# The second half of a quantized feed-forward layer: chunk loads moved from ScalarE's DMA queue to SyncE's, with another ring of integers and another split of the rounding

## The chip, the cores and the metric

The kernel runs on one core of a Trainium2 chip (trn2). The metric is the device time of one execution in microseconds; less is better. Five engines run their own instruction streams in order: TensorE (PE, its weight loads PEld), VectorE (DVE), ScalarE (ACT), GpSimd (POOL) and SyncE (SP). SP computes nothing; it issues DMAs. ACT can issue DMAs too. An instruction that waits holds up everything behind it on its engine, and this holds for SP's queue as well.

## The reference, cut to what matters

Two batches of 2048 tokens with 512 features pass through four residual steps. The last one, `_L1_ffn_ref`, is the part concerned:

```python
def act_quant(x):
    scale = 127.0 / jnp.clip(jnp.max(jnp.abs(x), axis=-1, keepdims=True), 1e-05)
    return jnp.clip(jnp.round(x * scale), -128, 127) / scale
...
h = bit_linear(x, w1)                 # 512 -> 2048, ternary weights
h = depthwise_conv1d(h.transpose(0, 2, 1), conv_w, conv_b)   # three taps along the tokens
h = h.transpose(0, 2, 1)
h = jax.nn.silu(h)
return bit_linear(h, w2)              # 2048 -> 512, ternary weights
...
x = x + jnp.tanh(g_xattn[1]) * _L1_xattn_ref(_layernorm(x, axis=-1), ctx_768, ...)
x = x + jnp.tanh(g_ffn[1]) * _L1_ffn_ref(_layernorm(x, axis=-1), ...)
```

`bit_linear` quantizes each token's row to integers of at most 127 before it multiplies. The scale of the second `bit_linear` needs the largest absolute value over all 2048 hidden features of a token, so nothing of a token's second half can be quantized until its whole first half is known.

## The kernel before

Tokens go in eight blocks of 512, g0 to g7, four to a batch (`NBLK` = 4, `LAST` = 7). The hidden features go in 16 chunks of 128 (`HC` = 16); a chunk of a block is a tile of 128 features by 512 tokens.

Beside the last attention (stage 3) runs the **first half** of each block, `first_half(g)`: for each chunk four matmuls (L1002), a scaling on DVE (L1012), the middle tap of the convolution on ACT (L1014), the two outer taps on DVE (L1018), all in `convolved`. After four chunks ACT applies Silu (L1043), SP stores the 1 MB of four chunks to DRAM (`h_d[g]`, L1049), ACT takes the absolute value in place (L1050, which must wait for that store), and DVE folds the maximum (L1051 to L1056). `quantize_rows(g)` makes the block's input: normalize and scale the four x3 tiles (ACT L968 and L978, DVE L971 and L980 into `xi`), and transpose them on PE (L986). g7 is not stored: its four-chunk tiles stay in SBUF (`kept`).

`scales_of(g)` turns the maxima into scales: a PE transpose (L1073), a DVE reduction (L1075) and five DVE instructions on four columns. For g0 to g3 (`EARLY` = 4) the integers are made during the attention by `integers(g)` and stored as bf16 in `hq_d[g]`. For g4 to g7 `quantize_hidden(g)` makes them in the second half.

The **second half** of a block, from `second_half_starts()` on, is in `down_and_out`: for each of the block's four row tiles 16 matmuls with the integers as weights (L1232), DVE scales and adds the residual (L1235), SP stores the result (`out_x`, L1236). Residual rows come from `x3_d` by `row_tile` (L1162); since the convolution lags one token, the first row tile of each batch (g0 and g4) has 127 rows, and its load and its store are DMAs of 127 rows.

`quantize_hidden(g)` before the change: for g0 to g3 it loads eight bf16 tiles of two chunks (`hq`, 256 KB each, L1198, by SP). For g4 to g6 it loads two chunks at a time (512 KB, L1188) by ACT's queue into six `h5` buffers, four loads ahead; multiplies by the scale spread over the partitions (`s_b`, one buffer, written by ACT at L1086) on DVE, every fourth on POOL (L1207); then rounds by adding and subtracting a large constant, odd ones on ACT in two steps (L1212, L1213), even ones on DVE in one (L1215). The integer tiles lie in two sets of eight, by the block's parity. `xr` holds eight x3 buffers, which in stage 3 carry the attention's residual rows, four to a block.

The order on each engine is not the program's: a scheduler places each instruction, and all waits go through semaphores. DMAs of SP and ACT take turns in eight completion slots; a DMA waits until the one eight before it has landed.

Of the kernel before, what the change touches and what calls it, by code (L numbers as in the profile page):

```python
# [10 lines left out]
F32 = mybir.dt.float32  # L11
BF16 = mybir.dt.bfloat16
AF = mybir.ActivationFunctionType
ALU = mybir.AluOpType
# [3 lines left out]
P = 128  # L18
B, S, D = 2, 2048, 512
NT = B * S // P  # L20
TPB = S // P
BLK = 512
TB = BLK // P
NBLK = S // BLK
# [8 lines left out]
HC = HID // P  # L33
# [5 lines left out]
def row_tiles(ap):  # L39
    return ap.rearrange("(c p) n -> p c n", p=P)  # L40
# [3 lines left out]
def flamingo_kernel(ctx: ExitStack, tc: tile.TileContext, a: dict, out: bass.AP):  # L44
    nc = tc.nc
# [4 lines left out]
    def psum_pool(stack, name, bufs):  # L50
        return stack.enter_context(tc.tile_pool(name=name, bufs=bufs, space=PSUM))
# [340 lines left out]
    with ExitStack() as st:  # L392
# [17 lines left out]
            out=before,  # L410
            in_=before,
# [9 lines left out]
            out=after,  # L421
            in_=after,
# [174 lines left out]
    with ExitStack() as st:  # L597
        AHEAD = 3
        wst = st.enter_context(tc.tile_pool(name="wst", bufs=AHEAD))
        keepp = st.enter_context(tc.tile_pool(name="keepp", bufs=1))  # L600
        w13 = {}

        def load_ffn(f):
            n = min(P, DFF - f * P)
            w1c = wst.tile([P, DC, P], F32, name="w1c", tag="w1c")
            nc.sync.dma_start(
                out=w1c[:, :, :n], in_=row_tiles(a["W1T"])[:, :, ds(f * P, n)]
            )
            w2c = wst.tile([P, DC, P], F32, name="w2c", tag="w2c")
            nc.sync.dma_start(  # L610
                out=w2c[:, :, :n], in_=row_tiles(a["W2T"])[:, :, ds(f * P, n)]
            )
            w3c = wst.tile([P, D], F32, name="w3c", tag="w3c")
            nc.sync.dma_start(out=w3c[:n, :], in_=a["W3T"][ds(f * P, n), :])
            w13[f] = (w1c, w2c, w3c)
# [28 lines left out]
        with ExitStack() as sa:  # L644
# [9 lines left out]
            for n in range(3):  # L654
                nc.sync.dma_start(
                    out=wqkv[:, :, ts(n, D)], in_=row_tiles(a["WqkvT"])[:, :, ts(n, D)]
                )
            wout = w.tile([P, DC, D], F32, name="wout")
            nc.sync.dma_start(out=wout, in_=row_tiles(a["WoutT"]))
            for f in range(AHEAD):  # L660
                load_ffn(f)
# [131 lines left out]
        with ExitStack() as sf:  # L793
# [64 lines left out]
            def down(f):  # L858
                n = min(P, DFF - f * P)
                for i in range(4):  # L860
                    nc.tensor.matmul(  # L861
                        acc[i],
                        gT[f][:n, ts(i, P)],
                        w13[f][2][:n, :],
                        start=(f == 0),
                        stop=(f == NF - 1),
                    )

            for f in range(NF):
# [16 lines left out]
                if f > 0:  # L886
                    down(f - 1)
                    if f - 1 + AHEAD < NF:
                        load_ffn(f - 1 + AHEAD)
                if f == 1:  # L890
# [8 lines left out]
            for i in range(4):  # L899
# [3 lines left out]
                    out=x_d[i // 2][:, :],  # L903
                    out_offset=bass.IndirectOffsetOnAxis(ap=idx[:, i : i + 1], axis=0),
                    in_=xa[i],
# [14 lines left out]
    GC = 4  # L920
# [7 lines left out]
    h_d = [dramp.tile([P, HC, BLK], F32, name=f"h_d{g}") for g in range(B * NBLK)]  # L928
    LAST = B * NBLK - 1
# [7 lines left out]
    xr = s4.enter_context(tc.tile_pool(name="xr", bufs=8))  # L937
# [4 lines left out]
    def quant_scale(mx, name, s=None):  # L942

        m = row4.tile([P, TB], F32, name=name + "m", tag="qm")
        nc.vector.tensor_scalar(m, mx, 1e-5, None, ALU.max)
        if s is None:
            s = row4.tile([P, TB], F32, name=name + "s", tag="qs")
        nc.vector.reciprocal(s, m)
        nc.vector.tensor_scalar(s, s, 127.0, None, ALU.mult)
        inv = row4.tile([P, TB], F32, name=name + "i", tag="qi")  # L950
        nc.vector.reciprocal(inv, s)
        return s, inv
# [42 lines left out]
    carry, ending, kept, act5 = {}, [], [], []  # L995
# [70 lines left out]

    def scales_of(g, amax):

        for _ in range(3):
            yield  # L1070
        pm = ps_mm.tile([P, TB, P], F32, name="pm", tag="mm")
        for i in range(TB):
            nc.tensor.transpose(pm[:, i, :], amax[:, ts(i, P)], ident)  # L1073
        mx = row4.tile([P, TB], F32, name="mxh", tag="mx4")
        nc.vector.tensor_reduce(mx, pm, AX.X, ALU.max)  # L1075
        _, inv = quant_scale(mx, "hq", hid_s[:, ts(g, TB)])
        nc.vector.tensor_scalar(hid_f[:, ts(g, TB)], inv, finstep, None, ALU.mult)
        if g < EARLY:
            later.append(integers(g))

    def scales_spread(g):

        pb = ps_mm.tile([P, BLK], F32, name="pb5", tag="mm")
        bcast_rows(pb, hid_s[:, ts(g, TB)], ident)
        s_b = act4.tile([P, BLK], F32, name="s_b", tag="s_b", bufs=1)
        nc.scalar.copy(s_b, pb)  # L1086
        return s_b
# [29 lines left out]
    def beside4(u, share=2):  # L1117


        for _ in range(share):  # L1120
            advance(ending)
            advance(stream)
        if u is None or u % 4 != 1:
            advance(later)
# [23 lines left out]


    w5, ps_5, quantizing, ahead = [], [], [], []  # L1150
    GQ, hq, used = 2, {}, []

    def row_tile(g, i):

        t = w5[0].tile([P, D], F32, name="x5w", tag="x5w", bufs=2)
        if g + i > 1:
            t = act5[0].tile([P, D], F32, name="x5", tag="x5", bufs=8)
        r, p = g % NBLK * BLK + i * P - 1, 0
        if r < 0:
            nc.sync.dma_start(out=t[0:1, :], in_=x3_d[g // NBLK][0:1, :])  # L1160
            r, p = 0, 1
        nc.sync.dma_start(out=t[p:, :], in_=x3_d[g // NBLK][ds(r, P - p), :])  # L1162
        return t, r, p

    def second_half_starts():
        units.close()
        w5.append(s4.enter_context(tc.tile_pool(name="w5", bufs=1)))
        w5.append(w5[0].tile([P, HC, D], BF16, name="w2q"))
        quantizing.append(quantize_hidden(0))
        nc.sync.dma_start(out=w5[1], in_=w2_d)  # L1170
        ps_5.append(psum_pool(s4, "s5_o", 4))
        next(quantizing[0], None)
        ahead.extend(row_tile(0, i) for i in range(2))

    def quantize_hidden(g):

        NK = HC // GQ
        hq[g] = []

        def load(k):  # L1180
            if g == LAST:
                return kept[k * GQ // GC][:, ds(k * GQ % GC, GQ), :]
            pool = (act5 if len(used) % 3 else w5)[0]
            used.append(g)
            h = pool.tile(
                [P, GQ, BLK], F32, name="h5", tag="h5", bufs=4 if pool is act5[0] else 2
            )
            nc.scalar.dma_start(out=h, in_=h_d[g][:, ts(k, GQ), :])  # L1188
            return h

        def integer_tile():
            pool = act5[0] if g % 2 else w5[0]
            hq[g].append(pool.tile([P, GQ, BLK], BF16, name="hq", tag="hq", bufs=NK))
            return hq[g][-1]

        if g < EARLY:
            for k in range(NK):
                nc.sync.dma_start(out=integer_tile(), in_=hq_d[g][:, ts(k, GQ), :])  # L1198
            return
        AHEAD = 4  # L1200
        hs = [load(k) for k in range(AHEAD)]
        s_b = scales_spread(g)
        yield
        for k in range(NK):
            h = hs.pop(0)
            eng = nc.gpsimd if k % 4 == 3 else nc.vector
            eng.tensor_tensor(  # L1207
                h, h, s_b.unsqueeze(1).to_broadcast([P, GQ, BLK]), ALU.mult
            )
            q = integer_tile()  # L1210
            if k % 2:
                nc.scalar.activation(h, h, AF.Copy, bias=RND)  # L1212
                nc.scalar.activation(q, h, AF.Copy, bias=-RND)  # L1213
            else:
                nc.vector.tensor_scalar(q, h, RND, RND, ALU.add, ALU.subtract)  # L1215
            if k + AHEAD < NK:
                hs.append(load(k + AHEAD))
            yield

    cross_attention(  # L1220
        W1, act, hold, ps_mm, psum_pool(units, "L1_sc", 3), psum_pool(units, "L1_o", 2), row,
# [52 lines left out]
    for g in range(LAST + 1):  # L1274
        if g == LAST - 1:
            while stream or ending:
                beside4(None)
            last_tokens()
        behind = quantize_hidden(g + 1) if g < LAST else iter(())
        for i in range(TB):  # L1280
            t, r, p = ahead.pop(0)
            down_and_out(
                lambda c: hq[g][c // GQ][:, c % GQ, ts(i, P)],
                hid_f[:, g * TB + i : g * TB + i + 1],
                P,
                t,
                out[ds(g // NBLK * S + r, P - p), :],
                p,
            )
            if g < LAST:  # L1290
                ahead.append(row_tile(g + 1, i))
            for _ in range(3):
                next(behind, None)
                beside4(None, 1)
# [65 lines left out]
```

## Time and profile before

| what | value |
|---|---|
| median of 3 runs | 1890.75 us (1885.45 to 1895.94) |
| profiled execution | 1896.89 us, its span 1892.8 us |
| mean TensorE clock granted | 0.945 |
| first L1012 of g7's first half | 1739.1 us after the start of the span |
| first L1207 (g4) | 1790.8 us |
| h loads by ACT | 24 of 512 KB, median 6.0 us from issue to landing |
| x5 and residual row loads by SP | 60 of 256 KB, median 5.1 us |
| L1207 on DVE, on POOL | 24 of 1479 ns, 8 of 2957 ns |
| L1212 and L1213 on ACT | 16 of 1052 ns, 16 of 1054 ns |

A group line of the profile reads: line, engine, operation, output <- input (partitions x elements, type), count | busy us, mean ns of one | idle time of the engine just before these instructions, with what ended it. A stretch line reads: from:to, length, then for each engine busy us and count, the granted TensorE clock, the DMA engines' busy share, and GB/s. In the views the tiles `x3` and `x5` both appear as `x`, `x3_d` and `x_d` as `x_d`, and `h5` as `h`.

### The profile page before, as it was taken

What the parts mean: (1) busy time and instruction counts of PE and PEld (TensorE: products, weight loads), DVE (VectorE), ACT (ScalarE), POOL (GpSimd) and SP (SyncE); (2) the same over time, 40 slices, a digit from 0 to 9 for tenths busy, and PEclk for the clock granted to TensorE, in tenths of its full rate; (3) what the DMA queues carried; (4) which work ended last, traced back from release to release, by engine and by line L of the source; (5) the groups of instructions that cost most, each with busy time, mean ns of one, the idle gap of its engine ahead of it and who ended that gap; (6) DMA issues with size and microseconds to landing.
All of it is one profiled execution on the core that took longest, in us unless ns stands there. A gap on an engine that the chain in (4) does not pass through costs nothing.

```text
span 1892.8 us, 24174 instructions
## 1 busy us (share of the span) xinstructions
PE 1684.2 (89%) x7580; PEld 841.7 (44%) x7626; DVE 1312.3 (69%) x2713; ACT 1041.1 (55%) x3021; POOL 554.0 (29%) x676
## 2 busy tenths in 40 slices
PE   6989988888837989989999999999999999887877
PEld 4544544444313543445544444445444444433433
DVE  5777898878772432224447789799798789675956
ACT  1645545355402635205547778788787779643523
POOL 4534343343202310032214242323234233221212
PEclk9999999899958989999999999999999999898989
DMA  7011011011122019330011134234243133157463
GB/s 281 1 45 46 1 46 45 12 45 46 45 94 100 1 62 347 110 89 23 29 40 62 78 117 142 98 123 150 75 143 101 78 103 131 36 210 239 154 220 127
DMA packets 94998, 184.33 MB, mean 97 GB/s; under 512 B 10944, under 2 KB 30144, under 8 KB 91159
## 3 DMA queue, kind: packets, MB, share of 16 engines
q1 hardware_dynamic: 90518, 168.11, 25.5%
q10 hardware_dynamic: 3456, 12.58, 2.0%
q0 software_dynamic: 896, 2.10, 0.6%
q8 instruction: 60, 0.98, 0.2%
q14 instruction: 68, 0.55, 0.1%
HBM read 108.31 MB, written 74.45 MB: 97 GB/s over the span
## 4 chain that ended last, share of the span: by engine, by line
PE 37%; DVE 12%; DMA 6%; ACT 4%; issue 2%; POOL 2%; SPq 1%; ACTq 0%; DVEq 0%; POOLq 0%
PE pp L315 9%; PE pq L248 8%; PE ph L1002 3%; PE po L297 3%; PE sc L271 3%; DVE h L1018 2%; PE pu L875 2%; PE tp L289 2%; PE po L1232 2%; PE acc L861 2%; PE pw L875 2%; DMA h<-h_d 1%; DVE h L1207 1%; DMA out_x<-x 1%; DMA out_x<-x5w 1%
## 5 line engine op out<-in xcount | busy, mean ns | idle before, releaser
L128 POOL TENSOR_TENSOR A<-A,rden 128x512 f32<-128x512 f32 x280 | 298.2, 1067 | 552.4 <-DVE rden L127 448.6
L119 ACT ACTIVATE A<-sc,nmx 128x128 f32<-128x128 f32 x1024 | 362.8, 377 | 168.5 <-DVE nmx L116 145.8
L315 PE MATMUL pp<-L_wo,OT 128*128 128x512 f32 x768 | 366.1, 611 | 10.2 <-DVE x L324 6.8
L248 PE MATMUL pq<-xnT,L_wq 128*128 128x512 f32 x768 | 360.6, 616 | 0.0
L119 ACT ACTIVATION_READ_ACCUMULATOR A<-sc,nmx 128x1 f32 x1024 | 221.4, 216 | 0.0
L248 PEld LDWEIGHTS pq<-xnT,L_wq 128*128 128x128 f32 x768 | 146.1, 197 | 161.2 <-issue 153.3
L116 DVE TENSOR_REDUCE nmx<-sc 128x4 f32<-128x512 f32 x256 | 169.1, 677 | 67.1 <-PE sc L271 66.8
L290 DVE COPY AT<-tp 128x512 f32<-128x512 f32 x256 | 172.9, 677 | 56.5 <-PE tp L289 56.0
L315 PEld LDWEIGHTS pp<-L_wo,OT 128*128 128x128 f32 x768 | 138.9, 195 | 157.8 <-issue 135.1
L1018 DVE SCALAR_TENSOR_TENSOR h<-u,cw,h 128x512 f32<-128x512 f32 x256 | 190.7, 779 | 6.0 <-ACT h L1014 5.5
L289 PE MATMUL tp<-ident,A 128*128 128x128 f32 x1024 | 164.5, 283 | 28.3 <-POOL A L128 26.7
L271 PE MATMUL sc<-L_kT,qT 32*128 32x128 f32 (+1 forms) x2048 | 163.5, 290 | 5.8 <-ACT A L119 5.1
L271 PEld LDWEIGHTS sc<-L_kT,qT 32*128 32x128 f32 (+1 forms) x2048 | 130.4, 188 | 85.5 <-issue 60.8
L289 PEld LDWEIGHTS tp<-ident,A 128*128 128x128 f32 x1024 | 119.7, 143 | 103.0 <-issue 47.5
L1232 PE MATMUL po<-w2q,hq 128*128 128x512 bf16 x501 | 125.9, 406 | 37.6 <-DMA hq<-hq_d 12.8
L1014 ACT ACTIVATE h<-u,cb,cw 128x512 f32<-128x512 f32 x128 | 99.1, 809 | 59.3 <-DVE u L1012 52.3
L1002 PE MATMUL ph<-xiT,w1q 128*128 128x512 bf16 x477 | 122.4, 380 | 6.0 <-DVE u L1012 3.9
L297 PE MATMUL po<-AT,L_v 128*32 128x512 f32 (+1 forms) x512 | 118.8, 634 | 9.4 <-DVE AT L290 9.0
L305 ACT COPY OT<-po 128x512 f32<-128x512 f32 x96 | 55.8, 588 | 103.2 <-PE po L297 102.7
L1012 DVE TENSOR_TENSOR u<-ph,inv_b 128x512 f32<-128x512 f32 x128 | 85.0, 682 | 33.0 <-PE ph L1002 26.1
L1011 POOL COPY u<-carry 128x2 f32<-128x2 f32 x128 | 49.1, 386 | 200.1 <-DVE h L1018 171.7
L1232 PEld LDWEIGHTS <-hq 128*128 128x128 bf16 x512 | 51.2, 103 | 108.9 <-issue 23.4
(218 smaller groups left out, 2266.3 us busy)
## 6 DMA issues: line engine op xcount, KB each, us to landing
h_d<-h SPq DMA_DIRECT2D x28, 1024.0 KB, 4.1
x_d<-x SPq DMA_DIRECT2D x64, 256.0 KB, 2.0
hf<-h_d SPq DMA_DIRECT2D x64, 256.0 KB, 3.0
x<-x_d SPq DMA_DIRECT2D x60, 256.0 KB, 5.1
h<-h_d ACTq DMA_DIRECT2D x24, 512.0 KB, 6.0
x<-in_x SPq DMA_DIRECT2D x32, 256.0 KB, 5.4
xn_d<-xn SPq DMA_DIRECT2D x32, 256.0 KB, 2.2
xf<-x_d SPq DMA_DIRECT2D x32, 256.0 KB, 3.0
```

What stands on the lines that cost most here:

```text
L116: nc.vector.tensor_reduce(nmx, sc, AX.X, ALU.max, negate=True)
L119: nc.scalar.activation(out_tile[:, h, :], sc[:, h, :], AF.Exp, bias=nmx[:, h : h + 1], accum_out=den[:, h : h + 1],)
L128: nc.gpsimd.tensor_tensor(out_tile, out_tile, rden.unsqueeze(2).to_broadcast([P, n, width]), ALU.mult,)
L248: nc.tensor.matmul(pq, W.wq[:, d, ts(e, P)], xnT[:, d, :], start=(d == 0), stop=(d == DC - 1),)
L271: nc.tensor.matmul(sc[h][:, t, :], qT[e % cpg][r, ts(t, P)], W.kT[r, b, e, :], start=True, stop=True,)
L289: nc.tensor.transpose(tp[:, t, :], A[:, t, :], ident)
L290: nc.vector.tensor_copy(AT, tp.rearrange("p t n -> p (t n)"))
L297: nc.tensor.matmul(po[h * dh : (h + 1) * dh, :], W.v[:, b, ts(hd, dh)], AT[c * hpc + h], start=True, stop=True,)
L315: nc.tensor.matmul(pp, OT[e][:, ts(i, P)], W.wo[:, e, :], start=(e == 0), stop=(e == nE - 1),)
L1002: nc.tensor.matmul(ph, w1q[:, d, ts(c, P)], xiT[g][:, d, :], start=(d == 0), stop=(d == DC - 1),)
L1018: nc.vector.scalar_tensor_tensor(z, u[:, ds(k, BLK)], cw[:, c, k : k + 1], z, ALU.mult, ALU.add)
L1232: nc.tensor.matmul(po, rows(c), w2q[:, c, :], start=(c == 0), stop=(c == HC - 1))
```

## The change

The integers of g0 and g1 are both requested when the second half starts, g1's second four tiles at the generator's next step. Integer tiles come from one ring of 24 (three blocks), twelve in each of two pools. For g4 to g6, single chunks (256 KB) are loaded by SP into the `x3` buffers, six ahead. All scaling is on DVE in tiles of 512, for g7 too. Of four chunks, one is rounded on DVE and three on ACT. `scales_of(6)` waits 16 turns of its generator instead of 3. The condition on where the first row tiles lie takes in the block size.

```diff
     def scales_of(g, amax):
-        for _ in range(3):
+        for _ in range(3 if g != LAST - 1 else HC):
             yield
...
-    GQ, hq, used = 2, {}, []
+    GQ, hq = 2, {}
+    next_integers = iter(range(B * NBLK * HC // GQ))
 
     def row_tile(g, i):
         t = w5[0].tile([P, D], F32, name="x5w", tag="x5w", bufs=2)
-        if g + i > 1:
+        if g * TB + i > 1:
             t = act5[0].tile([P, D], F32, name="x5", tag="x5", bufs=8)
...
-        quantizing.append(quantize_hidden(0))
         nc.sync.dma_start(out=w5[1], in_=w2_d)
         ps_5.append(psum_pool(s4, "s5_o", 4))
-        next(quantizing[0], None)
+        quantizing.extend(quantize_hidden(g) for g in range(2))
+        for q in quantizing:
+            next(q, None)
         ahead.extend(row_tile(0, i) for i in range(2))
 
     def quantize_hidden(g):
-        NK = HC // GQ
         hq[g] = []
-        def load(k):
-            if g == LAST:
-                return kept[k * GQ // GC][:, ds(k * GQ % GC, GQ), :]
-            pool = (act5 if len(used) % 3 else w5)[0]
-            used.append(g)
-            h = pool.tile(
-                [P, GQ, BLK], F32, name="h5", tag="h5", bufs=4 if pool is act5[0] else 2
-            )
-            nc.scalar.dma_start(out=h, in_=h_d[g][:, ts(k, GQ), :])
-            return h
-
         def integer_tile():
-            pool = act5[0] if g % 2 else w5[0]
-            hq[g].append(pool.tile([P, GQ, BLK], BF16, name="hq", tag="hq", bufs=NK))
+            pool, bufs = (w5[0], 12) if next(next_integers) % 24 < 12 else (act5[0], 12)
+            hq[g].append(pool.tile([P, GQ, BLK], BF16, name="hq", tag="hq", bufs=bufs))
             return hq[g][-1]
 
         if g < EARLY:
-            for k in range(NK):
+            for k in range(HC // GQ):
+                if g == 1 and k == HC // GQ // 2:
+                    yield
                 nc.sync.dma_start(out=integer_tile(), in_=hq_d[g][:, ts(k, GQ), :])
             return
-        AHEAD = 4
-        hs = [load(k) for k in range(AHEAD)]
+
+        def load(c):
+            if g == LAST:
+                return kept[c // GC][:, c % GC, :]
+            h = xr.tile([P, D], F32, name="x3", tag="x3")
+            nc.sync.dma_start(out=h, in_=h_d[g][:, c, :])
+            return h
+
+        AHEAD = 6
+        hs = [load(c) for c in range(AHEAD)]
         s_b = scales_spread(g)
         yield
-        for k in range(NK):
+        for c in range(HC):
             h = hs.pop(0)
-            eng = nc.gpsimd if k % 4 == 3 else nc.vector
-            eng.tensor_tensor(
-                h, h, s_b.unsqueeze(1).to_broadcast([P, GQ, BLK]), ALU.mult
-            )
-            q = integer_tile()
-            if k % 2:
+            nc.vector.tensor_tensor(h, h, s_b, ALU.mult)
+            q = (integer_tile() if c % GQ == 0 else hq[g][-1])[:, c % GQ, :]
+            if c % 4:
                 nc.scalar.activation(h, h, AF.Copy, bias=RND)
                 nc.scalar.activation(q, h, AF.Copy, bias=-RND)
             else:
                 nc.vector.tensor_scalar(q, h, RND, RND, ALU.add, ALU.subtract)
-            if k + AHEAD < NK:
-                hs.append(load(k + AHEAD))
-            yield
+            if c + AHEAD < HC:
+                hs.append(load(c + AHEAD))
+            if c % 2:
+                yield
...
-        behind = quantize_hidden(g + 1) if g < LAST else iter(())
+        behind = quantizing[1] if g == 0 else quantize_hidden(g + 1) if g < LAST else iter(())
```

## The prediction, on record before the result

> **What bounds the kernel now.** I read the page's busy row, then the stretch table, then the chain of waits, then the timelines at the chain's gaps. The busy row names TensorE:
>
> ```profile
> PE 1684.2 (89%) x7580; PEld 841.7 (44%) x7626; DVE 1312.3 (69%) x2713; ACT 1041.1 (55%) x3021; POOL 554.0 (29%) x676
> ```
>
> That is an average. The edits touch only what runs after about 1640 us, so the stretch table of that part decides:
>
> ```profile
> core 0: us, PE busy (x) PEld busy (x) DVE busy (x) ACT busy (x) POOL busy (x), PEclk, DMA share, GB/s
> 1720.00:1725.00 5.00, 0.63 (x2) 0.21 (x3) 0.00 (x0) 0.25 (x1) 0.00 (x0) 0.50 0.14 40
> ...
> 1760.00:1770.00 10.00, 9.63 (x45) 4.31 (x44) 9.76 (x16) 5.62 (x6) 2.45 (x8) 1.00 0.24 90
> ...
> 1820.00:1830.00 10.00, 4.00 (x11) 1.20 (x9) 2.06 (x3) 3.38 (x4) 0.00 (x0) 0.50 0.38 122
> ...
> 1790.80:1892.80 102.00, 73.53 (x292) 29.67 (x296) 63.66 (x71) 34.26 (x35) 23.61 (x8) 0.86 0.52 178
> ```
>
> Three regimes. Near 1720 no engine works and DMA is nearly idle. From 1739 to 1790 (first half of g7) PE and DVE are both full. In the last 102 us (g4 to g7 quantized and multiplied) no engine reaches three quarters, so waits bound that part. The chain of waits (start, us, what) says which:
>
> ```profile
> 1705.78 17.84 DMA out_x<-x5w
> 1725.43 6.56 DMA hq<-hq_d
> ...
> 1816.70 9.44 DMA out_x<-x
> 1826.21 6.50 DMA h<-h_d
> 1832.74 1.22 DVE h L1207
> ```
>
> Both places start with a store of 254 KB, the 127-row tile that opens a batch. The DMA view of 1718 to 1726, forty slices, shows what it does:
>
> ```profile
> GB/s 338 256 72 72 20 31 20 31 20 31 20 31 20 31 20 31 20 31 20 31 20 31 20 31 20 31 20 20 31 20 31 20 41 184 215 154 307 399 379 399
> ```
>
> For 5 us the core moves 25 GB/s where it moves up to 400 otherwise, a sixteenth: one DMA engine works alone. 254 KB at 25 GB/s is 10.2 us. The timelines of DVE and of ACT show who stands still (start, us, engine, line; in brackets the idle time before it):
>
> ```profile
> 1733.96 0.75 DVE L1235 SCALAR_TENSOR_TENSOR x5w<-po,hid_f,x5w 128x512 f32<-128x512 f32 x1 [15.09 <-PE po L1232]
> 1826.59 1.06 ACT L1213 ACTIVATE hq<-h 128x1024 bf16<-128x1024 f32 x1 [8.05 <-DMA out_x<-x]
> ```
>
> In the first, DVE stands 15.1 us at g1's first output row, because five of g1's eight loads stood on SP behind that store; three of g7's four xi (L980) are queued behind it on DVE, so g7's first half starts only at 1739.1. In the second, ACT, which issues the h loads itself, stands 8 us at an issue.
>
> **What the Trainium skill says.** (1) "DMA: Bandwidth & Descriptors", section on why a DMA increments its semaphore by 16: the number of engines is the largest up to 16 that divides the slowest dimension, so 127 partitions run on one. The 25 GB/s agree. (2) The same page, "Issuing engines are not separate DMA queues": moving loads from ACT to SP saves issue time on ACT and gives no bandwidth. The trace agrees that an issue can cost ACT more than its 0.33 us: the 8 us above. (3) "SBUF — State Buffer", "Who interferes with whom": a DVE instruction with two SBUF inputs contends with a GpSimd one that reads SBUF. L1207 on DVE takes 2.2 to 3.3 us beside the GpSimd one and 1.22 us otherwise; it agrees. (4) "VectorE: DVE Perf Modes", section on the TRN2 errata: SBUF-source instructions of VectorE and ScalarE pay a fixed time each, so halving tiles costs. The groups agree: ACT takes 634 ns for 512 elements and 1052 for 1024.
>
> **The change, part by part.** Rows for the prices:
>
> ```profile
> L1207 DVE TENSOR_TENSOR h<-h,s_b 128x1024 f32<-128x1024 f32 x24 | 34.8, 1479 | 17.2 <-DMA h<-h_d 13.2 <-ACT s_b L1086 4.0
> L1207 POOL TENSOR_TENSOR h<-h,s_b 128x1024 f32<-128x1024 f32 x8 | 23.6, 2957 | 67.2 <-DMA h<-h_d 54.0 <-ACT s_b L1086 13.1
> L1212 ACT ACTIVATE h<-h 128x1024 f32<-128x1024 f32 x16 | 16.7, 1052 | 41.4 <-DVE h L1207 21.1 <-POOL h L1207 20.3
> L1215 DVE TENSOR_SCALAR hq<-h 128x1024 bf16<-128x1024 f32 x16 | 14.2, 910 | 0.0
> L1104 ACT ACTIVATE hf<-hf 128x512 f32<-128x512 f32 x32 | 20.3, 634 | 16.0 <-DVE hf L1101 15.4 <-DVE xqs L948 0.5
> ```
>
> *Engine work of g4 to g7.* Scaling: 24 on DVE and 8 on POOL become 64 of 512 on DVE. One takes 0.62 (L1012 back to back, 1.87 for three) to 0.76 us (mean of L1101, beside POOL work); with POOL idle I take 0.62, 39.7 us for 35 before. Rounding on DVE: 16 of 512 at 0.38 (L980: 1.08 for three), 6 us for 14. So DVE has no more to do, and POOL's 23.6 us vanish. Rounding on ACT: 32 of 1024 (33.4 us) become 96 of 512; 0.55 overlapped to 0.63 alone; I take 0.58, 56 us. Per block that is DVE 16 x 0.62 + 4 x 0.38 + 4 outputs x 0.67 = 14.1, ACT 24 x 0.58 + 0.6 = 14.5, PE 64 x 0.22 = 14.1 us (47 of L1232 take 10.52 us at 1701.9): level, where before they waited.
>
> *Loads.* 24 of 512 KB on ACT become 48 of 256 KB on SP, through the 8 x3 buffers. SP issues each in 0.4 us: 24 more instructions, 10 us of a queue that mostly waits. In the order laid down, four chunks of g4 go ahead of the w2q load, when SP is idle (before: 31 us of waiting, 1622 to 1653.8), and four more before g7's first half ends: 8 of g4's 16 chunks are in place. Later loads wait for a buffer: about 4 us to land (bounds: hf 3.0 on the page, x5 rows 6.1 in the DMA view from 1600 us on), 0.7 on DVE, 2 to 3 for ACT, so 7.5 us per 8 chunks, 0.94 each or 15 us a block: as fast as the engines, no faster.
>
> *Output rows on the same SP queue.* Before, ACT's loads met stores through shared completion slots. Now chunk loads stand directly behind out_x stores that wait for DVE, which waits for PE. The worst is g4's 127-row store, placed before g5's chunk 8. It occupies one DMA engine for 10.2 us, and every later load has a sixteenth of its rows there.
>
> *g1 loaded earlier, ring of three.* 6 of 8 tiles of g1 now stand ahead of the 127-row store of g0; tiles 7 and 8 directly behind it, and g2's after an x5 load that waits for it to land. PE's transposes of xi stand between matmuls of tile 6 and tile 8. On DVE all four xi now come before g1's first output. So the start of g7's first half waits for that store still, but for one term only. The store goes out at 1704 to 1706; ahead of it on the lone engine lie three x5 loads, two hq, one h_d store and one row store, 2.5 MB, 6.6 us at the 380 GB/s of 1660 to 1665, or already partly drained; then 10.2 us; then a tile share of 0.7 us: tiles 7 and 8 at 1719 to 1724. Before, the last tile came at 1732.0. I take **12 us** (bounds 3, if the store is late, and 15, the whole DVE stall).
>
> *Before that.* 12 hq loads instead of 6 precede g6's second h_d store, whose L1050 on ACT waited 9.8 us (again a 127-row load ahead of it). That store goes out at about the same time; four ACT steps now precede the wait, not two. 0 to 6 us gained; already inside the 12.
>
> *Delay of scales_of(6).* Its reduction and scales (0.69 + 5 x 0.17 us) and 6 more matmuls of g1 (6 x 0.22) move into the full stretch: +1.5 us, no cover there.
>
> *Sum for the last stretch*, from the first L1207, T: g4 15.5; last_tokens on DVE 3.7; g5 until chunk 8 is needed T+27.5, stalled by the store (out at T+21) to T+32.5, end T+40.5; s_b change 1.3; g6 16.2 (T+58); 1.3; g7 on DVE to T+72.5; PE has 37 matmuls of g6 and 64 of g7 left after g6's last rounding, 101 x 0.22 = 22 us: T+82; last L1235 and store, 3.8 as now: **T+86**, 16 less than 102.
>
> Total: 12 - 1.5 + 16 = 26.5 off the profiled execution's 1896.89 (span 1892.8 + 4.1). That one is 6.1 above the median 1890.75, so I predict 1890.75 - 26.5 = **1864 us**.
>
> **Rivals.** *Ring or SP as the bound, ending slower.* If a turn of the 8-buffer ring takes R us, 40 loaded chunks take 5 R: stretch = 6 (g4's first 8) + 5 R + 28 (g6's end to the last store). DVE decides up to R = 10; all gains are gone at R = 15.7; R = 18 gives 124 us, so 1902. For it: one queue, stores ahead of loads, out_x landings up to 14.1 us. Against: the late stretch moves 178 GB/s at half DMA share. 6%.
> *Store still covers g1.* If tiles 7 and 8 land at 1730, 9 us of the 12 are lost: 1873; with ACT at 0.63 and ring stalls of 2 us a block 1882. For it: same lone engine, same place. 16%.
> *Lone engine hidden.* If g5's chunks are ahead enough and PE trails less, the stretch is DVE's sum, 72 to 75 us: 1848. For it: eight preloaded chunks. 24%.
> *The stall moves wholly.* 40 chunks (10 MB) and some 20 row tiles in and out (5 MB) wait in one line, both gains halve or vanish: 1882 to 1895. 9%.
> My forecast, 1855 to 1876, has 45%.
>
> **How the numbers follow.** A measurement can tell about 0.5% (9.5 us) from no change. Forecast, lone engine hidden and most of the third case lie below 1881.3: faster 0.85; same 0.08; slower 0.07. Range 1842 (lone engine hidden, phase gains at their bounds) to 1883.
>
> **What would show it.** Right: L1207 absent from POOL; no DMA issue on ACT; the first L1012 of g7 near 1726; DVE idle 3 to 8 us before a chunk of g5, ended by DMA; last stretch near 86 us. Wrong: the 15 us stall on DVE or PE still there, DVE waiting for DMA in every block, or ACT busy over nine tenths and last in the chain.

## The result, and the profile after

The changed kernel takes 1870.2 us (median of 4 runs, 1868.1 to 1878.9) where the kernel before took 1891.6 beside it: a ratio of 0.989, 95% interval 0.985 to 0.993. Forecast were 1864 us and a range of 1842 to 1883. The profiled execution took 1878.9 us, its span 1877.2.

The busy row of the page after (engine, busy us, share, instructions):

```profile
PE 1684.7 (90%) x7580; PEld 845.9 (45%) x7626; DVE 1306.7 (70%) x2753; ACT 1063.0 (57%) x3085; POOL 529.8 (28%) x668
```

It has hardly moved, and POOL has lost its scaling. To see where time went, both traces need a common mark, because the work ahead of the edited part doesn't take the same time in every execution: the last softmax exponential (L119) of the third attention starts at 1643.6 us before and at 1651.0 after. From this mark the rest falls into three stretches: to g7's first L1012, to the first L1207, to the end. The stretch table of before (the start alone) and then of after (from:to, length, busy us and count of each engine, granted TensorE clock, DMA share, GB/s):

```profile
1643.60:1739.10 95.50, 76.40 (x269) 32.60 (x274) 57.54 (x101) 41.04 (x48) 15.29 (x34) 0.89 0.55 198
```

```profile
1651.00:1732.30 81.30, 71.43 (x258) 32.01 (x262) 56.22 (x94) 40.87 (x48) 15.05 (x34) 0.94 0.55 195
1732.30:1785.30 53.00, 51.35 (x238) 23.56 (x242) 49.33 (x84) 27.62 (x26) 12.13 (x29) 1.00 0.51 178
1785.30:1877.20 91.90, 71.00 (x298) 28.96 (x302) 59.93 (x112) 55.33 (x99) 0.00 (x0) 0.90 0.61 206
```

The start went from 95.5 to 81.3, the full stretch from 51.7 to 53.0, the last from 102.0 to 91.9: together -23.0, near the -21.4 of the medians. The spans differ by 15.6 only, since this execution reached the mark 7.4 us late.

PE still stands idle for 9.9, 1.7 and 20.9 us in them. The chain of waits after (start, us, what) names the three places:

```profile
1711.17 15.69 DMA hq<-hq_d
...
1774.30 8.18 DMA out_x<-x
...
1809.57 12.90 DMA x<-h_d
```

Each lies behind a DMA of 127 rows: g0's first store (issued at 1710.9), g4's first residual load (1768.9) and g4's first store (1809.2). The DMA view of 1808 to 1824, forty slices, has the floor seen in the kernel before, 26 GB/s, in its first part and again late:

```profile
GB/s 348 399 399 220 26 15 15 15 10 15 5 20 26 26 26 41 169 328 328 379 353 312 184 220 297 307 333 333 364 405 251 123 36 26 26 26 26 164 276 246
```

The timelines of PE and DVE show who pays (in brackets the idle time before, and what ended it):

```profile
1799.21 14.44 PE L1231 MATMUL po<-w2q,hq 128*128 128x512 bf16 x52 [5.99 <-ACT hq L1211]
...
1824.29 12.92 PE L1231 MATMUL po<-w2q,hq 128*128 128x512 bf16 x48 [7.85 <-DVE hq L1213]
```

```profile
1795.42 0.69 DVE L1207 TENSOR_TENSOR x<-x,s_b 128x512 f32<-128x512 f32 x1 [4.31 <-DMA x<-h_d]
...
1822.50 1.40 DVE L1207 TENSOR_TENSOR x<-x,s_b 128x512 f32<-128x512 f32 x2 [8.37 <-DMA x<-h_d]
```

What PE waited for here are roundings; those waited for L1207, and L1207 for a chunk. The groups of the new work (us busy, mean ns, idle before) give the prices that the prediction had to guess; scaling in place of L1207's two old rows, rounding on ACT, rounding on DVE:

```profile
L1207 DVE TENSOR_TENSOR x<-x,s_b 128x512 f32<-128x512 f32 x48 | 31.3, 686 | 17.3 <-DMA x<-h_d 15.4 <-ACT s_b L1086 1.8
L1211 ACT ACTIVATE hq<-x 128x512 bf16<-128x512 f32 x36 | 21.1, 618 | 0.3
L1213 DVE TENSOR_SCALAR hq<-x 128x512 bf16<-128x512 f32 x12 | 5.0, 417 | 0.0
```

These means include overlap with the next instruction: four L1207 in a row take 2.49 us, 0.62 each.

### The profile page after: what moved, and what is told of

Its sections match the earlier page's. It is cut to its first block, busy times and chain, and to the rows that moved or that the text cites. A ratio compares the mean times of both kernels' runs of the same rounds, so it can differ in the third digit from the quotient of the medians.

```text
span 1877.2 us, 24320 instructions
## 1 busy us (share of the span) xinstructions
PE 1684.7 (90%) x7580; PEld 845.9 (45%) x7626; DVE 1306.7 (70%) x2753; ACT 1063.0 (57%) x3085; POOL 529.8 (28%) x668
## 4 chain that ended last, share of the span: by engine, by line
PE 36%; DVE 12%; DMA 6%; ACT 5%; issue 2%; POOL 2%; SPq 1%; POOLq 0%; DVEq 0%; ACTq 0%
PE pp L315 9%; PE pq L248 8%; PE ph L1002 3%; PE po L297 3%; PE sc L271 2%; DVE h L1018 2%; PE pu L875 2%; PE tp L289 2%; PE po L1231 2%; PE acc L861 2%; PE pw L875 2%; DMA x<-h_d 1%; DVE u L1012 1%; ACT A L119 1%; DVE AT L290 1%
## 5 line engine op out<-in xcount | busy, mean ns | idle before, releaser
L119 ACT ACTIVATE A<-sc,nmx 128x128 f32<-128x128 f32 x1024 | 363.4, 377 | 175.6 <-DVE nmx L116 151.3
L119 ACT ACTIVATION_READ_ACCUMULATOR A<-sc,nmx 128x1 f32 x1024 | 220.0, 215 | 0.0
L1231 PE MATMUL po<-w2q,hq 128*128 128x512 bf16 x501 | 120.9, 393 | 19.6 <-ACT hq L1211 8.4
L1002 PE MATMUL ph<-xiT,w1q 128*128 128x512 bf16 x477 | 123.4, 382 | 3.0 <-DVE u L1012 0.6
L1012 DVE TENSOR_TENSOR u<-ph,inv_b 128x512 f32<-128x512 f32 x128 | 85.1, 684 | 30.8 <-PE ph L1002 26.3
L311 POOL TENSOR_TENSOR x<-x,L_bo 128x512 f32<-128x512 f32 x64 | 87.0, 1377 | 38.0 <-DMA x<-x_d 15.8
```

The lines of the kernel that those rows point to most:

```text
L119: nc.scalar.activation(out_tile[:, h, :], sc[:, h, :], AF.Exp, bias=nmx[:, h : h + 1], accum_out=den[:, h : h + 1],)
L1002: nc.tensor.matmul(ph, w1q[:, d, ts(c, P)], xiT[g][:, d, :], start=(d == 0), stop=(d == DC - 1),)
L1231: nc.tensor.matmul(po, rows(c), w2q[:, c, :], start=(c == 0), stop=(c == HC - 1))
```

## Experiments

All are compared with the kernel before on the same chip. The three stretches are those of above, from one profiled execution each.

| kernel | us | ratio to before, 95% | start | full | last |
|---|---|---|---|---|---|
| before | 1891.6 | 1 | 95.5 | 51.7 | 102.0 |
| changed | 1870.2 | 0.989 (0.985 to 0.993) | 81.3 | 53.0 | 91.9 |
| b_store112 | 1868.9 | 0.988 (0.986 to 0.991) | 82.6 | 51.8 | 89.5 |
| b_both112 | 1861.4 | 0.984 (0.982 to 0.985) | 75.6 | 51.8 | 94.5 |
| a_store112 | 1858.0 | 0.983 (0.980 to 0.986) | 77.8 | 52.9 | 83.2 |
| a_both112 | 1840.8 | 0.974 (0.971 to 0.977) | 70.0 | 52.9 | 75.4 |
| b_g1_early | 1893.8 | 1.002 (1.000 to 1.003) | 98.0 | 52.5 | 99.0 |
| b_cond | 1889.1 | 0.999 (0.997 to 1.000) | 91.8 | 51.7 | 100.6 |
| a_late | 1867.4 | 0.987 (0.985 to 0.989) | 78.3 | 53.1 | 90.9 |
| a_cond_undone | 1872.0 | 0.990 (0.988 to 0.992) | 83.1 | 52.9 | 91.3 |
| a_act_queue | 1884.3 | 0.996 (0.994 to 0.997) | 82.3 | 53.1 | 105.9 |
| a_split | 1840.9 | 0.973 (0.972 to 0.975) | 66.7 | 53.0 | 77.5 |
| a_split_pool | 1857.5 | 0.983 (0.980 to 0.985) | 66.7 | 53.0 | 90.8 |
| a_split_round2 | 1847.9 | 0.978 (0.975 to 0.980) | 67.0 | 53.0 | 84.6 |

### The lone DMA engine, in both kernels

The edit for the stores, in the changed kernel (a_store112) and in the one before (b_store112):

```diff
-        nc.sync.dma_start(out=to, in_=t[p:, :])
+        nc.sync.dma_start(out=to[0:112, :] if p else to, in_=t[1:113, :] if p else t)
```

and for the loads besides (a_both112, b_both112):

```diff
-            nc.sync.dma_start(out=t[0:1, :], in_=x3_d[g // NBLK][0:1, :])
+            nc.sync.dma_start(out=t[0:16, :], in_=x3_d[g // NBLK][0:16, :])
...
-        nc.sync.dma_start(out=t[p:, :], in_=x3_d[g // NBLK][ds(r, P - p), :])
+        nc.sync.dma_start(out=t[16 * p :, :], in_=x3_d[g // NBLK][ds(r + 15 * p, P - 16 * p), :])
```

No engine's order changes, only the size of these DMAs. These four kernels leave out 15 output rows of each batch, so they serve to measure and not to be used.

> The changed kernel, with the two stores of 127 rows cut to their first 112 rows (15 output rows of each batch are left out); every engine's order stays as it is. Theory 'lone engine': a DMA of 127 rows runs on one DMA engine for about 10 us, and all that is issued behind it has a share in that engine's line. With 112 rows the store takes 2 to 3 us. Expected: the last hq tiles of g1 land near 1719 instead of 1726.9, the first L1012 of g7 goes from 1732.3 to about 1726 (-6); in g5 the wait of DVE for a chunk falls from 8.4 us to under 1.5, and the last stretch (first L1207 to the end) from 91.9 to about 85 (-6): 1870 becomes 1858, 1853 to 1862. Rival 'one line': the loads are late because they stand behind other loads and stores in SP's queue and because the x3 buffers come free late; store size does not matter: 1867 to 1871, the 8.4 us wait stays over 6. Rival 'next bound': the stalls go, but PE and DVE, full in g7's first half and nearly full later, take back what is won in the first place: only one of the two gains is kept, 1863 to 1866.

> As the run with stores of 112 rows, and the two loads of 127 rows become 112 rows, the single-row load ahead of each 16 rows (15 residual rows of each batch come one token off); every engine's order stays as it is. Theory 'lone engine': the third stall (from the load of 127 rows at 1769 on, SP stands until 1782.5, g4's chunks from the ninth on land at 1795, DVE idle 4.3 + 1.2 and PE 6.0 us) goes as well: another 5 us beyond the stores alone, 1853 in all (1848 to 1858), and no wait of DVE for a chunk of g4 over 1.5 us. Rival 'one line': chunk nine of g4 comes late because x3 buffers and SP's order hold it, not the load: no difference from the run with the stores alone (within 2 us), DVE still waits 4 us for it. Rival 'next bound': chunks come earlier but PE's backlog sets the end: 0 to 2 us.

> The kernel before, with the two stores of 127 rows cut to 112 rows (15 output rows of each batch left out); order unchanged. Theory 'lone engine': the 15.1 us stall of DVE near 1720 shrinks to about 6 (the tile that came at 1732.0 comes about 8 us earlier), g7's first L1012 from 1739.1 to about 1731, and the 8.05 us hold of ACT at an issue near 1820 falls under 2, worth 4 to 8 in the last stretch: 1891 becomes 1878 (1872 to 1883), about half of what the whole change brought. Rival 'one line': 1888 to 1893. Rival 'the load is what covers': the stall keeps more than 10 us because the x5w load of 127 rows at about 1676 already shifted the rest, first L1012 of g7 at 1737 or later: 1884 to 1888.

> The kernel before, with the stores and the loads of 127 rows cut to 112 rows (15 output rows of each batch left out, the single-row load takes 16 rows, 15 residual rows come one token off); order unchanged. With the stores alone it took 1868.9; the changed kernel with both took 1840.8. Theory 'both': the lone engine and the engines' work per block are two separate losses. The loads are worth 6 to 10 here too (L1050 of g6 waits 10.1 us for a store queued behind the x5w load), so 1860 (1855 to 1865), and the change is still worth about 20 without any lone engine (scaling on GpSimd, ACT issuing loads: the last stretch near 88 against 75). Rival 'only the lone engine': what the change brought was a better order around the DMAs of 127 rows; without them both kernels are level: 1840 to 1848. Rival 'the load is hidden': 1866 to 1870.

The stores alone bring 12.2 us in the changed kernel, as the lone-engine theory had it, and 22.3 in the one before, where 13 were expected: b_store112 is level with the whole change. With the loads too, the changed kernel takes 1840.8 us; 1853 was expected, so the loads are worth 17 us and not 5. The kernel before takes 1861.4, as the theory "both" had it (1860). DVE's waits in the last stretch, changed kernel and then a_both112 (engine, line, waited for: us in total, times, longest):

```profile
DVE x L1207 <- DMA x<-h_d: 15.4, 6, 8.4
```

```profile
DVE x L1207 <- DMA x<-h_d: 2.1, 4, 0.6
```

PE fills most of its time once the chunks come (a_both112, the start and the last stretch):

```profile
1639.60:1709.60 70.00, 67.37 (x258) 30.28 (x262) 56.05 (x95) 40.99 (x48) 16.11 (x34) 1.00 0.66 238
...
1762.50:1837.90 75.40, 66.93 (x298) 26.98 (x302) 59.67 (x112) 55.34 (x99) 0.00 (x0) 1.00 0.68 235
```

The rivals "one line" and "next bound" fall: the DMAs' size alone takes the stalls away, and both gains are kept. Set side by side, the lone engine costs each kernel 30 us (1891.6 to 1861.4, 1870.2 to 1840.8), and the change is worth about 21 with it and 21 without. So the change does not gain in sum by getting out of that engine's way. By stretches it does: in the start it loses less to it (11.3 us for 19.9), in the last more (16.5 for 7.5). Without the lone engine the change is worth 5.6 us in the start and 19.1 in the last, where with it the two are 14.2 and 10.1.

### What moved the start: the early request, or the condition on row tiles

b_g1_early is the kernel before with the early request alone:

```diff
-        quantizing.append(quantize_hidden(0))
...
-        next(quantizing[0], None)
+        quantizing.extend(quantize_hidden(g) for g in range(2))
+        for q in quantizing:
+            next(q, None)
...
+            early = g == 1 and len(hq[g]) < 4
+            pool = w5[0] if early or g % 2 == 0 else act5[0]
+            hq[g].append(pool.tile([P, GQ, BLK], BF16, name="hq", tag="hq1" if early else "hq", bufs=4 if early else NK))
...
+                if g == 1 and k == 4:
+                    yield
...
-        behind = quantize_hidden(g + 1) if g < LAST else iter(())
+        behind = quantizing[1] if g == 0 else quantize_hidden(g + 1) if g < LAST else iter(())
```

a_late is the changed kernel without it, the ring kept:

```diff
-        quantizing.extend(quantize_hidden(g) for g in range(2))
+        quantizing.extend(quantize_hidden(g) for g in range(1))
...
-                if g == 1 and k == HC // GQ // 2:
-                    yield
...
-        behind = quantizing[1] if g == 0 else quantize_hidden(g + 1) if g < LAST else iter(())
+        behind = quantize_hidden(g + 1) if g < LAST else iter(())
```

> The kernel before, with one part of the change alone: g1's integers requested with g0's, the first four tiles into four more buffers; the six h5 buffers all lie in the later pool for it, and x5 has seven buffers instead of eight. g4 to g7 are quantized as before. Theory: this part alone moves the start of g7's first half by what the changed kernel shows, 1739.1 to about 1732 (-7), and the last stretch stays at 102 +- 3: 1884 (1880 to 1889). Rival 'split gain': the earlier loads only help with the new chunk order behind them, because the scheduler's order of the phase differs: under 3 us, 1888 to 1894. Rival 'as first worked out': -12, 1876 to 1880.

> The changed kernel with g1's integers requested when g0's rows go out, as before the change, ring of three kept; with it four of g1's eight tiles stand behind the store of 127 rows again (three in the kernel before stood ahead of it). Anchor: the last softmax exponential (L119). From it the first L1012 of g7 came at 95.5 us before, 81.3 after. Theory 'early request': it is what moved that start; here it comes at 89 to 95, and the time is 1878 (1874 to 1884); the last stretch stays at 92. Rival 'other parts': the 14 us came from ACT no longer issuing loads and from the place of g6's last h_d store and of its maximum's transposes (L1073), the early request being worth nothing, as it was alone on the kernel before: 80 to 84 from the anchor, 1868 to 1872.

Both went against the theory. Alone, the early request gains nothing; taken out, nothing is lost (78.3 us to g7's first L1012, where 89 to 95 were expected). In b_g1_early seven of g1's eight tiles do stand ahead of the store, but another wait takes the place of theirs. Its chain, and its PE timeline:

```profile
1697.89 18.89 DMA h_d<-h
1716.86 1.92 ACT h L1050
```

```profile
1722.07 1.12 PE L1073 MATMUL pm<-ident,amax 128*128 128x128 f32 x4 [14.25 <-DVE amax L1056]
```

g6's last h_d store now went out behind the 127-row store, so its L1050 and g6's maximum were late, and PE stood 14.3 us at L1073 with 29 matmuls of g1 queued behind. Without those 14.3 us its start would be about 84 (98.0 less 14.3, an estimate).

The SP timeline of the kernel before (start, us, line) then showed what the prediction had misread, and the expectation of a_late too, which had three of g1's tiles ahead of the store. All eight stood behind it: three directly, which took SP 9.8 us, and five behind an x5w load, the third tile in two buffers:

```profile
1705.78 0.30 SPq L1236 DMA_DIRECT2D out_x<-x5w  x1
1706.29 9.79 SPq L1198 DMA_DIRECT2D hq<-hq_d  x3
1723.64 0.32 SPq L1162 DMA_DIRECT2D x5w<-x_d  x1
1724.00 2.33 SPq L1198 DMA_DIRECT2D hq<-hq_d  x5
```

That load waited until the store of 1705.8 (17.84 us) was done with its buffer. The condition `g * TB + i > 1` in the diff removes this wait: only two tiles lie in x5w now. b_cond makes that edit alone on the kernel before; a_cond_undone takes it back in the changed one:

```diff
-        if g + i > 1:
+        if g * TB + i > 1:
```

> The kernel before with one condition of the change alone: only the first two row tiles lie in the two x5w buffers, g1's first row in an x5 buffer. On PE, ACT and POOL the order is unchanged; on SP the load of g1's first row goes ahead of g1's last five integer tiles without waiting for a store. Theory 'buffer': in the kernel before that load waited for the x5w buffer which the store of 127 rows (17.84 us) was reading, and SP stood with five loads behind it until 1723.6. Without it the last tile lands about 8 to 12 us earlier; from the last L119 the first L1012 of g7 comes at 80 to 87 instead of 95.4, the last stretch stays at 102 +- 3: 1892 becomes 1880 (1876 to 1884). Rival 'store covers': the tiles go out earlier, but a sixteenth of each stands behind the store on its one DMA engine: 91 to 93, 1888 to 1891. Rival 'PE's own wait': L1073 or g6's last h_d store takes its place: 93 to 96, 1890 to 1894.

> The changed kernel with that condition alone as before the change: g1's first row again in the two x5w buffers. The early request stays, and now all of g1's tiles stand ahead of the waiting load, only g2's behind it. Theory 'substitutes': condition and early request do the same work, so one can go: 81 us from the anchor to g7's first L1012 as in the changed kernel, +-3, 1866 to 1874. Rival 'condition carries it all': the stores and x5 loads that stand behind the waiting load hold DVE and PE: 88 to 95, 1876 to 1884.

b_cond has the size of the rival "store covers": 91.8 us, 2.5 us in all. SP stands still, just at another instruction, the one behind the store of 1706.1:

```profile
1707.81 8.14 SPq L1162 DMA_DIRECT2D x<-x_d  x1
1716.00 10.17 SPq L1198 DMA_DIRECT2D hq<-hq_d  x8
```

The load behind the 127-row store takes SP 8.1 us by itself, and all eight tiles of g1 stand behind it; PE waits 9.5 us for the first. a_cond_undone lies within "substitutes" (83.1, 1872.0). So of the start's 14 us no single one of these two edits is the cause: undone singly they cost 2 us at most, alone they gain 4 at most. The issuing queue is not it either (a_act_queue: 82.3).

The SP timelines tell the kernels apart by how many of g1's eight tiles go out ahead of g0's 127-row store: none before and in b_cond, four in a_late, six in the changed kernel, seven in a_cond_undone and in b_g1_early. In the changed kernel (the nine are five tiles of g0 and four of g1):

```profile
1668.07 8.13 SPq L1191 DMA_DIRECT2D hq<-hq_d  x9
...
1708.16 0.90 SPq L1191 DMA_DIRECT2D hq<-hq_d  x2
...
1710.87 0.26 SPq L1235 DMA_DIRECT2D out_x<-x5w  x1
1711.17 7.50 SPq L1191 DMA_DIRECT2D hq<-hq_d  x2
```

and in a_late:

```profile
1673.88 4.91 SPq L1191 DMA_DIRECT2D hq<-hq_d  x4
...
1702.98 0.26 SPq L1235 DMA_DIRECT2D out_x<-x5w  x1
...
1708.75 3.00 SPq L1191 DMA_DIRECT2D hq<-hq_d  x4
```

In the changed kernel, a_late and a_cond_undone PE gets g1's last tile 75.9 to 77.7 us from the mark, where it came at 88.4 before. So a_late takes back when g1 is requested, but not that some of its tiles go early: the first twelve tiles of the ring lie in a pool that opens during the attention, while before the change all of g1's lay in one that opens after it. b_g1_early has the tiles early too and loses the gain at L1073. In the changed kernel g6's last h_d store goes out ahead of the 127-row store (1709.2 and 1710.9), and L1073 comes at 1732.1, behind g7's first L1002, where it can't hold PE; the delay of `scales_of(6)` is the edit that bears on its place. The traces speak for both together, tiles of g1 ahead of the store and L1073 out of the way. But neither the ring of three nor the delay was taken back by itself, nor the four early chunk loads, so this is argued, not shown.

### The queue of the chunk loads

```diff
             h = xr.tile([P, D], F32, name="x3", tag="x3")
-            nc.sync.dma_start(out=h, in_=h_d[g][:, c, :])
+            nc.scalar.dma_start(out=h, in_=h_d[g][:, c, :])
```

> The changed kernel with the chunk loads of g4 to g6 issued by ACT instead of SP; sizes, buffers and rounding as in the changed kernel; DMAs of 127 rows as they are. Theory 'held issue': 48 issues of 0.33 to 0.4 us (16 us on an engine that has 55 us of work in the last stretch of 92) and the waits for a free x3 buffer hold ACT's rounding: +5, 1875 (1871 to 1882), ACT idle before L1210 or L1211 ended by a DMA. Rival 'SP's line': chunk loads no longer stand behind stores that wait for DVE, so they go out earlier: 1860 to 1867. Rival 'neutral': the lone engine sets the end in either case, 1868 to 1871.

1884.3 us, 14 more than the changed kernel, in the last stretch alone (105.9 for 91.9). ACT's waits there:

```profile
ACT hq L1211 <- DMA out_x<-x: 16.7, 2, 12.8
...
ACT hq L1211 <- DMA x<-x_d: 6.4, 3, 4.1
```

ACT can't round while it stands at the issue of a load that waits for an earlier transfer; L1211 stands behind it. 23 us of such waits are more than the issues themselves, 40 of 0.33 us, 13 in all. "Held issue" is right, and it was under-priced (5 expected). The longest wait, 12.8 us, falls while the 127-row store of 1810.7 is under way, so a part of the 14 us is again the lone engine's; the move was not tried without it. With the loads on ACT, the rest of the new quantizing (smaller chunks, all scaling on DVE, three of four roundings on ACT) leaves the last stretch at 105.9, against 102.0 before the change.

### A complete kernel without the lone engine, and the split of the work in it

a_split writes and reads all rows, in 112 + 15:

```diff
-        nc.sync.dma_start(out=t[p:, :], in_=x3_d[g // NBLK][ds(r, P - p), :])
+        for a, b in ((p, 113), (113, P)) if p else ((0, P),): nc.sync.dma_start(out=t[a:b, :], in_=x3_d[g // NBLK][ds(r + a - p, b - a), :])
...
-        nc.sync.dma_start(out=to, in_=t[p:, :])
+        for a, b in ((p, 113), (113, P)) if p else ((0, n),): nc.sync.dma_start(out=to[a - p : b - p, :], in_=t[a:b, :])
```

> The changed kernel, complete, with each DMA of 127 rows as one of 112 and one of 15 rows. The scheduler moves some instructions for it. Theory 'lone engine': as the run with 112 rows both ways, plus four SP issues of 0.4 us and what the other order costs: 1843 (1838 to 1850), 2.5% under the kernel before. Rival 'small pieces cost': a DMA of 15 rows takes nearly as long as one of 127 rows, so the stalls stay at half their length: 1853 to 1860. Rival 'order': the moved instructions lose 5 us or more, with no chunk wait over 2 us on DVE: 1848 to 1856.

1840.9 us: 2.7% under the kernel before (ratio 0.973, 0.972 to 0.975), 1.6% under the changed one by the medians. Both pieces are short. Its stretches show PE busy for most of the time:

```profile
1646.40:1713.10 66.70, 64.81 (x249) 29.01 (x249) 54.77 (x93) 40.90 (x48) 15.53 (x34) 1.00 0.64 231
...
1766.10:1843.70 77.60, 69.71 (x316) 28.50 (x314) 59.57 (x112) 55.19 (x100) 0.00 (x0) 0.98 0.68 234
```

With 51.8 of 53.0 us in the stretch between, PE works 186 of 197 us. On this kernel, two parts of the change were taken back: every fourth scaling on GpSimd, and every second chunk rounded on DVE.

```diff
-            nc.vector.tensor_tensor(h, h, s_b, ALU.mult)
+            (nc.gpsimd if c % 4 == 3 else nc.vector).tensor_tensor(h, h, s_b, ALU.mult)
```

```diff
-            if c % 4:
+            if c % 2:
```

> The changed kernel with its DMAs of 127 rows in two pieces (1840.9) and every fourth chunk of g4 to g7 scaled on GpSimd again. Theory 'PE bound': PE works 186 of the last 197 us there, so relieving DVE by 16 x 0.62 = 10 us brings nothing and slower chunks cost nothing: 1838 to 1844. Rival 'late chunk': the matmuls take the chunks in order, and a GpSimd chunk (half of 2.3 to 3.4 us) comes 0.6 to 1 us later and slows DVE's beside it: 16 times 0.5 us, 1846 to 1852.

> As the kernel with two pieces (1840.9), with every second chunk rounded on DVE instead of every fourth. DVE gets 16 x 0.38 = 6 us more in the last stretch of 77 (66 of 77), ACT 16 x 1.16 = 19 less (36 of 77). Theory 'PE bound': no difference, 1838 to 1844. Rival 'DVE next': DVE's queue of scaling and rounding sets the chunks' pace, +4 to +7: 1845 to 1849. Rival 'shorter chain': one step on DVE instead of two on ACT feeds PE sooner at each block's start: 1834 to 1838.

Both are slower, by 16.5 and 6.9 us, and neither of my theories had the reason. In both the scheduler's order puts the 32 small matmuls of `last_tokens` on PE ahead of DVE's `ql` (L1258); first a_split_pool, then a_split_round2:

```profile
1812.96 8.51 PE L1231 MATMUL po<-w2q,ql 128*1 128x512 bf16 x32 [8.97 <-DVE ql L1258]
```

```profile
1805.34 8.84 PE L1231 MATMUL po<-w2q,ql 128*1 128x512 bf16 x32 [8.55 <-DVE ql L1258]
```

In a_split these matmuls wait for nothing:

```profile
1802.40 7.07 PE L1231 MATMUL po<-w2q,ql 128*1 128x512 bf16 x32
```

For the rounding this wait is larger than the 7.1 us by which the last stretch grew, so no cost of the split itself is seen. For GpSimd 4.3 of 13.3 remain, in line with the rows of L1207 there (ns min/median/max):

```profile
L1207 DVE TENSOR_TENSOR x<-x,s_b x36: 653/683/1761, 1764.4 to 1816.2; 128x512 f32<-128x512 f32 x36
L1207 POOL TENSOR_TENSOR x<-x,s_b x12: 1262/1567/1771, 1764.5 to 1815.8; 128x512 f32<-128x512 f32 x12
```

A chunk takes 1.57 us on GpSimd for 0.68 on DVE (medians), and one beside it on DVE up to 1.76: the contention that the Trainium skill describes ("SBUF — State Buffer", "Who interferes with whom"), now for single chunks. But with an 8 to 9 us wait by the order in each, these two runs don't settle what the split is worth.

## Why the prediction was right or wrong

- **Start, -12 us: the size and the landing were right, the reading of the stall was not, and which edit brings the gain is open.** From the mark the start went down by 14.2; g1's late tile landed 75.9 us after it, where 75.4 to 80.4 had been worked out, with six tiles ahead of the store and two behind, as forecast. But the prediction had five of g1's loads behind the store in the kernel before. All eight stood there, and the five waited for an x5w load, and so for the whole store; the diff's condition on row tiles, which removes that wait, was priced nowhere in the sum. Of the step "g1 loaded earlier, ring of three" the early request is worth nothing by itself (a_late, b_g1_early); the ring was not taken back.
- **Full stretch, +1.5 us: right.** It is 51.7 before and 52.9 to 53.1 in all kernels with the change; L1075 stands in it, at 1732.9. It was counted as pure cost; that it also keeps L1073 out of PE's way is argued above, not shown.
- **Last stretch, -16 us: 10.1.** Two terms were mis-sized. g5's stall behind the 127-row store was put at 5 us and took 8.4 on DVE. And the 127-row *load* at 1768.9 was not in the sum: SP, standing behind the stores and loads that it delayed, issued g4's ninth chunk only at 1792.4, and DVE lost 5.5 us (4.31 and 1.17), PE 6.0. "8 of g4's 16 chunks are in place" was right, but the other eight were not free. Together that is 8.9 us where the stretch missed by 5.9 (91.9 for 86): without its stall, g4 with the last tokens took 14.5 us, and 19.2 had been put.
- **Engine work per block: right.** 112 instructions take DVE 59.9 us in the last stretch, with 16 x 0.62 for the scaling as taken. The reading of L1207 beside GpSimd was off: 3.3 to 3.4 us in three of the 24 instructions before the change and 1.2 in all others, not 2.2 to 3.3, so the two engines met seldom. With the stalls gone the last stretch takes 75.4 us (a_both112), just over the 72 to 75 of the rival "lone engine hidden". That rival gave 1848 for the end; with no lone engine at all, it is 1841.
- **Issues off ACT: right, and worth more than they were given.** The sum gave them no term of their own; a_act_queue puts it at 14 us with the lone engine in place, more than the last stretch gained (10.1). The Trainium skill ("DMA: Bandwidth & Descriptors", "Issuing engines are not separate DMA queues") grants the issue time alone, "usually small relative to the DMA itself". That an issue can hold ACT for longer, where the prediction has trace and page agree, only the trace says: the waits came to 23 us, the issues to 13.
- **Rivals.** "Ring or SP as the bound, ending slower" did not come: the last stretch took 91.9 us, not over 102. A sign named for being wrong came weakly, though: DVE waited for chunks in each of g4, g5 and g6 (5.5, 8.4 and 1.5 us). "Store still covers g1" came in part: g1's late tile at 1726.9 stands in the chain of waits, and PE waited 2.3 us for it.
- **Sum.** -26.5 forecast, -23.0 measured from the mark, -21.4 in the medians. In part this is luck: the start came out 2.2 us better than its term and the last stretch 5.9 worse. Most of the signs named to tell it held: no L1207 on POOL, no issue on ACT, DVE idle before a chunk of g5 for 8.4 us (3 to 8 expected). The last stretch, to be near 86, was 91.9. The first L1012 of g7 is 1732.3 on this trace's clock; taking off the 7.4 us of the late mark, 1724.9 (1726 forecast).

## What to carry to other kernels

When a load is late, read the issuing queue instruction by instruction, and find which instruction holds the head. Then look past it to what it waits for: here the head waited for a buffer that a store was reading; with that wait gone (b_cond) the next load stood behind the same store and 2.5 us were won, while a store off the lone engine won 22 (b_store112). Look for DMAs whose row count has no large divisor up to 16: at four places, 112 and 15 rows instead of 127 were worth 29 us in the changed kernel, more than the whole change. And keep loads that may wait off an engine that computes: their price is its standing still (23 us here) more than the issue (13).

## What the runs showed of the hardware

- A DMA of 127 rows also holds its issuer. The 14 traces have 32 of them on SP. Behind 31 of these, the next DMA on SP or the one after it took 2.8 to 8.7 us to issue: 6.9 in the changed kernel (the first of the two at 1711.2), 8.1 in b_cond (1707.8), 5.4 in a_late (1703.3). From 1600 us on no other issue on SP took over 2.0 us, and the median of all is 0.34. In a_split two hq loads behind the two pieces took 2.1. It is not the wait for a completion slot: the slot of the 6.9 us issue had come free 1.8 us before it. So for up to 8.7 us nothing else goes out from SP.
- 127 rows as 112 + 15 cost little: the first store's two pieces in a_split took SP 2.0 us to issue, and no out_x store from 1690 us on took over 5.3 us to land, where in the changed kernel one took 9.5. The rule that the number of engines is the largest up to 16 dividing the rows (the Trainium skill, "DMA: Bandwidth & Descriptors", on why a DMA increments its semaphore by 16) fits all of these runs.
